# Graph attention on one core: a step's transposes and its running maximum are issued at other places

## The chip, the core and the metric

The kernel is one program on one core of a Trainium2 chip. The metric is device time in microseconds of one execution, given as the median of three runs. A profiled execution of the same program gives the trace that all views below are taken from. Engines: TensorE (PE for its matmuls, PEld for its weight loads), VectorE (DVE), ScalarE (ACT), GpSimd (POOL) and SyncE (SP).

## What is computed

Two layers over a graph of 10,000 nodes with 512 features and 160,000 edges `src -> dst`. Layer 0 is a mixture of four two-layer graph convolutions. Layer 1, where the change is, is graph attention with 8 heads of 64, followed by a feed-forward block. Cut to what matters:

```python
q, k, v = (z @ W.T + b for each)          # z = layernorm(x)
s = einsum('ehd,ehd->eh', q[src], k[dst]) / sqrt(64) + att_bias
m = segment_max(s, src);  p = exp(s - m[src])
alpha = p / segment_sum(p, src)[src]
agg = segment_sum(alpha * v[dst], src)
x = x + agg @ Wo.T + bo
x = x + silu(layernorm(x) @ W1.T + b1) @ W2.T + b2      # 512 -> 1024 -> 512
out = layernorm(layer_input + x)
```

## The kernel before, in words

The program runs three stages one after the other: the first convolutions, then the second ones with the projections to q, k and v, then attention with the feed-forward block. Only the third is touched. It starts at line 1459 of the kernel (`with ExitStack() as p3`).

**Tiling.** The nodes are cut into 79 blocks of 128 (`NB`). A block is worked off in four steps (`NQ`), each for a window of 32 nodes, so that there are 316 steps. A step `w` has block `b` and quarter `j = w % 4`. The edges of a window fill five columns of 128 slots (`CAP`): four of its own, and one that the block's windows share ("over"). For each column, GpSimd gathers 128 rows of key and value from `kv_all` with an indirect DMA (`pull`, L1552) into one of four buffers, two steps ahead. Softmax needs no exact maximum per node. The kernel takes one maximum per head and slot row, then one over all rows of the window, and subtracts that.

**The loop** (`for w in range(NW + 3)`) is a software pipeline whose order is written out by hand: `tc.manual_schedule` keeps PE, DVE, ACT and POOL in program order. A window goes through these stations:

- `expand` (L1793, TensorE): multiplies turned one-hots with the queries, so that each slot has its query row in PSUM. Two column pairs, groups 0 and 1. `expand_over` (L1801) does the same for the shared column in the last step of a block.
- `score` (L1845, DVE): queries times keys, one instruction of 128x1024 for each group. `score_over` is L1807 and L1810.
- L1882 (DVE): the sum over the 64 features of each head. Then `weigh` begins: L1695 (DVE) takes the maximum over the columns.
- `one`, the window's `weigh` in the next step. Four calls of `next(one, 1)`: L1697 (PE) turns the 128x8 maxima, L1700 (DVE, "last maximum") reduces the turned rows, L1702 (PE, two records, "its spread") multiplies the result with an identity so that all partitions hold it, and L1704 (DVE) subtracts it. The last call also issues the exponential L1707 and L1709 (ACT), and the first part of L1716 (POOL): probabilities times one-hots for columns 2 to 4, then L1721 (POOL).
- `two`, a step later: L1716 (DVE) does columns 0 and 1, L1730 (PE, 80 records of one step) forms the weighted sums, L1735/L1736 (DVE) and L1739 (ACT) divide.
- `three`, a step later still: L1741 (PE, "turned rows") turns the window's result, L1742 (ACT) copies it out. With a block's last window this call also puts the job `front(b)` at the head of the job list.
- `turn_hots(w + 2)`: four transposes L1576 (PE, "one-hots") and one copy L1579 (ACT), for the `expand` of the coming step. When `j == 2` a step begins with four more of the same kind, for the shared column of the next block (`over_t`).

L1697, L1702 and L1576 write to different columns of one PSUM bank, the tile `turns`.

**Dense work between.** What follows attention is put into jobs: `front(b)` (L1596 output projection, layer norm, L1620 transposes), `back` for two blocks (L1637, eight groups of four matmuls up, each followed by a Silu L1639 on ACT; L1647 down) and `tail` (L1655, L1659, last layer norm, L1662, store). `advance(rate)` gives jobs room: 2.6 us of dense TensorE work at the step's start (EARLY), 2.4 near its end (LATE), 0 in two places between, where only pieces without cost go on. A `back` job issues at most one group of L1637 in an `advance`. A step on TensorE before the change: EARLY pieces, L1697, expand group 0, L1702, the 80 weighted sums, expand group 1, L1741, L1576, LATE pieces.

ACT needs another function table for each of Exp (L1707), Silu (L1639) and Sqrt (L1679); an ACT_TABLE_LOAD at one of these lines is that switch.

Of the kernel before, what the change touches and what calls it, by code (L numbers as in the profile page):

```python
# [636 lines left out]
def fast(ctx: ExitStack, tc: tile.TileContext, a: dict, out: bass.AP, bad: bass.AP):  # L637
# [823 lines left out]
    with ExitStack() as p3:  # L1461
# [57 lines left out]
        def open_block(b):  # L1519
            if b >= NB:  # L1520
                return
            meta = dp.tile([P, SBC, WP], F32, name="meta", bufs=3)
            nc.sync.dma_start(meta, slots1[:, b * SBC:(b + 1) * SBC, :])
            oh = dp.tile([P, BC, 3, W], BF16, name="oh", bufs=3)
            mine = oh[:, :, 0, :].rearrange("p (q c) n -> p q c n", c=CAP)
            loc = meta[:, :SBC - 1, 1].rearrange("p (q c) -> p q c", c=SC_W)
            nc.vector.tensor_tensor(mine[:, :, :SC_W, :],
                                    loc[:, :, :, None].to_broadcast([P, NQ, SC_W, W]),
                                    iota_q[:, :, None, :].to_broadcast([P, NQ, SC_W, W]),
                                    op=ALU.is_equal)  # L1530
            nc.vector.tensor_scalar(mine[:, :, SC_W, :], iota_q, meta[:, SBC - 1, 1:2], None,
                                    op0=ALU.is_equal)
            nc.scalar.copy(oh[:, :, 1:, :], oh[:, :, 0:1, :].to_broadcast([P, BC, 2, W]))
            blocks[b] = meta, oh

        def open_query(b):
            if b < NB:
                q = dp.tile([3 * W, NQ, D], BF16, name="q")
                for t in range(3):
                    nc.sync.dma_start(q[t * W:(t + 1) * W],  # L1540
                                      q_all[b, t].rearrange("(j n) d -> n j d", n=W))
                queries[b] = q
# [15 lines left out]
        def pull_over(b):  # L1558
            if b < NB:
                fetch(kvo[b % 3], b, SBC - 1)  # L1560
# [9 lines left out]
        def turn_hots(w):  # L1570
            b, j = divmod(w, NQ)
            return turned(b, range(j * CAP, j * CAP + SC_W), "oh_t", 4)
# [182 lines left out]
        def advance(rate):  # L1755

            credit[0] = min(credit[0], 0.5) + rate
            for job in list(jobs):
                free = True
                while job.cost not in (None, STOP) and (  # L1760
                        free if job.cost == 0 else rate and credit[0] >= 0.5 * job.cost):
                    free = free and job.cost > 0
                    credit[0] -= max(job.cost, 0)
                    job.cost = next(job.steps, None)
                if job.cost == STOP:
                    job.cost = 0
                if job.cost is None:
                    jobs.remove(job)

        with tc.manual_schedule(engines={ET.PE, ET.DVE, ET.Activation, ET.Pool}):  # L1770
            for t in kvb[1:] + kvo[1:]:
                nc.vector.memset(t, 0.0)
            for b in range(2):
                open_block(b)
            open_query(0)
            pull_over(0)
            for w in range(KB):
                pull(w, range(SC_W))
            pull_over(1)
            over_t = {0: turned(0, range(SC_W, BC, CAP), "over_t", 2)}  # L1780
            hots = {w: turn_hots(w) for w in range(2)}
            one, two, three = iter(()), iter(()), iter(())
            qe, s_over = {}, {}

            GROUPS = [(0, 1), (2, 3)]

            def expand(w, g):

                if w < NW:
                    b, j = divmod(w, NQ)  # L1790
                    qe[w, g] = px.tile([P, 2, D], F32, name="qe")
                    for i, c in enumerate(GROUPS[g]):
                        nc.tensor.matmul(qe[w, g][:, i, :], hots[w][:, c, :], queries[b][:, j, :],  # L1793
                                         start=True, stop=True)

            def expand_over(b):

                if b < NB:
                    qe[b] = px.tile([P, 2, D], F32, name="qe")
                    for j in range(NQ):  # L1800
                        nc.tensor.matmul(qe[b][:, 0, :], over_t[b][:, j, :], queries[b][:, j, :],  # L1801
                                         start=(j == 0), stop=(j == NQ - 1))

            def score_over(b):
                if b < NB:
                    k = kvo[b % 3][:, :HV]
                    nc.vector.tensor_tensor(by_head(k), by_head(qe.pop(b)[:, 0, :]), by_head(k),  # L1807
                                            op=ALU.mult)
                    s = s_over[b] = dp.tile([P, H], F32, name="s_over")
                    nc.vector.tensor_reduce(s, k.rearrange("p (h d) -> p h d", h=H),  # L1810
                                            axis=AX.X, op=ALU.add)

            def bias_over(b):

                if b < NB:
                    nc.scalar.copy(kvo[b % 3][:, :HV].rearrange("p (h d) -> p h d", h=H)[:, :, DH],
                                   blocks[b][0][:, SBC - 1, 2:])

            expand_over(0)
            bias_over(0)  # L1820
            score_over(0)
            expand(0, 0)
            expand(0, 1)
            EARLY, LATE = 2.6, 2.4
            for w in range(NW + 3):
                b, j = divmod(w, NQ)
                kv = kvb[w % KB]
                last = j == NQ - 1
                if w < NW:
                    s = dp.tile([P, CAP, H], F32, name="s", bufs=3)  # L1830
                    nc.scalar.copy(s[:, SC_W, :], s_over[b])
                    nc.scalar.copy(
                        kv[:, :, :HV].rearrange("p c (h d) -> p c h d", h=H)[:, :, :, DH],
                        blocks[b][0][:, j * SC_W:(j + 1) * SC_W, 2:])
                if last:
                    bias_over(b + 1)
                if j == 2 and b + 1 < NB:
                    over_t[b + 1] = turned(b + 1, range(SC_W, BC, CAP), "over_t", 2)

                def score(g):  # L1840
                    if w < NW:
                        cs = GROUPS[g]
                        k = kv[:, cs[0]:cs[-1] + 1, :HV].rearrange("p c (h d) -> p c h d", h=H)
                        k = k[:, :, :, :DH]
                        nc.vector.tensor_tensor(  # L1845
                            k, qe.pop((w, g)).rearrange("p c (h d) -> p c h d", h=H), k,
                            op=ALU.mult)

                advance(EARLY)
                next(one, 1)
                score(0)
                next(two, 1)
                if last:
                    expand_over(b + 1)
                else:
                    expand(w + 1, 0)
                advance(0)  # L1860
                next(one, 1)
                score(1)
                next(one, 1)
                next(two, 1)
                expand(w + 1, 0 if last else 1)
                if last:
                    score_over(b + 1)
                if w >= 2:
                    pull(w - 2 + KB, range(SC_W))
                    if j == 0:  # L1870
                        pull_over(b + 1)
                next(one, 1)
                advance(0)
                next(three, 1)
                if w + 2 < NW:
                    hots[w + 2] = turn_hots(w + 2)
                if last:
                    expand(w + 1, 1)
                advance(LATE)
                first = iter(())  # L1880
                if w < NW:
                    nc.vector.tensor_reduce(s[:, :SC_W, :],  # L1882
                                            kv[:, :, :HV].rearrange("p c (h d) -> p c h d", h=H),
                                            axis=AX.X, op=ALU.add)
                    first = weigh(w, s)
                    next(first)
                next(two, 1)
                one, two, three = first, one, two
                if j == 1:
                    open_block(b + 2)  # L1890
                    open_query(b + 1)
                    open_rest(b)
            while jobs:
                advance(5.0)
# [57 lines left out]
```

## Time and profile before

| | |
|---|---|
| median of three runs | 11618.71 us (11617.09 to 11625.96) |
| profiled execution, its own time | 9845.47 us |
| its span, first to last instruction | 9843.6 us |
| mean granted TensorE clock in it | 0.987 |
| attention's 316 steps, first to last L1882 | 6986.8 to 9740.4 us, 8.74 us a step |
| in 7113 to 9740 us: PE, DVE, POOL, ACT busy | 92%, 88%, 75%, 68% |

The profiled execution is 15% shorter than the median of the runs, and lies 1.9 us around its span. The steps repeat in a cycle of eight (two blocks share one `back` job), and the cycle is steady: 36 cycles in the middle of the stage have lengths that agree within about 0.1 us. A step is 8.74 us on average, while the busiest engine is busy for 92% of it; so what counts is not a total but which wait ends last at each place of a step. In the views below, "<-" names what ended a wait. A line with PE has matmuls (a float32 matmul has two records), one with PEld the weight loads of the same instructions.

### The profile page before, as it was taken

What the parts mean: (1) busy time and instruction counts of PE and PEld (TensorE: products, weight loads), DVE (VectorE), ACT (ScalarE), POOL (GpSimd) and SP (SyncE); (2) the same over time, 40 slices, a digit from 0 to 9 for tenths busy, and PEclk for the clock granted to TensorE, in tenths of its full rate; (3) what the DMA queues carried; (4) which work ended last, traced back from release to release, by engine and by line L of the source; (5) the groups of instructions that cost most, each with busy time, mean ns of one, the idle gap of its engine ahead of it and who ended that gap; (6) DMA issues with size and microseconds to landing.
All of it is one profiled execution on the core that took longest, in us unless ns stands there. A gap on an engine that the chain in (4) does not pass through costs nothing.

```text
span 9843.6 us, 168369 instructions
## 1 busy us (share of the span) xinstructions
PE 9351.2 (95%) x63334; PEld 5440.1 (55%) x63334; DVE 5458.8 (55%) x8330; ACT 2943.9 (30%) x6062; POOL 6987.3 (71%) x6736
## 2 busy tenths in 40 slices
PE   7999999999999999899999999999799999999998
PEld 4666666666666667333333333333456565656565
DVE  7898992000100001355555555545788888888885
ACT  1111111111111111111111111111366666666665
POOL 5566666777777776677777777777577777777774
PEclk9999999999999999999999999999799999999999
DMA  6545445555555554788888888887788888888883
GB/s 216 179 153 158 156 158 158 160 157 162 158 162 163 160 165 132 262 299 297 294 303 301 291 298 297 299 302 274 227 273 278 272 275 271 272 274 270 272 276 125
DMA packets 1077230, 2263.26 MB, mean 230 GB/s; under 512 B 250526, under 2 KB 500260, under 8 KB 1075638
## 3 DMA queue, kind: packets, MB, share of 16 engines
q0 software_dynamic: 588224, 1659.68, 51.8%
q1 hardware_dynamic: 479456, 577.23, 17.0%
q10 hardware_dynamic: 8726, 15.49, 0.5%
q8 instruction: 502, 8.22, 0.3%
q14 instruction: 322, 2.64, 0.1%
HBM read 2181.26 MB, written 379.27 MB: 260 GB/s over the span
## 4 chain that ended last, share of the span: by engine, by line
PE 61%; DMA 10%; DVE 9%; ACT 8%; issue 7%; POOL 5%; POOLq 0%; ACTq 0%; DVEq 0%; SPq 0%
PE mm L1190 21%; PE mm L1200 11%; PE mm L1385 6%; DMA y<-y_tab,ix 5%; PE p_ag L1151 4%; PE bank L1647 3%; PE p_ag L1426 3%; DMA ring<-y_tab,ix 3%; PE bank L1637 2%; DVE m L930 2%; PE bank L1596 2%; POOL y L1330 2%; PE mm L1347 2%; DVE kv L1845 2%; PE sums L1730 2%
## 5 line engine op out<-in xcount | busy, mean ns | idle before, releaser
L1126 POOL DMA_INDIRECT ring<-in_x_dram,idx_t x1580 | 1901.2, 1203 | 1011.5 <-PE p_ag L1151 567.4
L1190 PE MATMUL mm<-tt,big 128*128 128x256 f32 (+1 forms) x8960 | 1964.7, 377 | 0.0
L1190 PEld LDWEIGHTS mm<-tt,big 128*128 128x128 f32 x8960 | 1680.5, 190 | 289.3 <-issue 71.3
L1060 POOL DMA_INDIRECT sorted<-pay,addr x1250 | 1278.0, 1022 | 380.5 <-issue 336.6
L1552 POOL DMA_INDIRECT kv<-kv_all,meta x948 | 965.4, 1018 | 515.6 <-PE sums L1730 276.6
L1330 POOL DMA_INDIRECT y<-y_tab,ix x920 | 950.4, 1033 | 287.2 <-issue 217.9
L1200 PE MATMUL mm<-wn,h 128*128 128x512 f32 x2528 | 1124.0, 597 | 0.0
L1385 PE MATMUL mm<-big,hb 128*128 128x512 f32 x2528 | 1120.4, 596 | 1.2 <-DMA hb<-h_tab 1.2
L1192 ACT ACTIVATE h<-mm,bl 128x256 f32<-128x256 f32 (+1 forms) x640 | 301.8, 472 | 2125.7 <-PE mm L1190 2125.7
L1330 POOL DMA_INDIRECT ring<-y_tab,ix x660 | 686.8, 1041 | 234.6 <-issue 162.7
L1347 PE MATMUL mm<-big,z_t 128*128 128x512 f32 x1896 | 829.2, 594 | 0.7 <-ACT z_t L1340 0.7
L1388 DVE TENSOR_TENSOR mine<-mm,bias 128x512 f32<-128x512 f32 x316 | 218.6, 692 | 1075.4 <-PE mm L1385 1074.9
L1385 PEld LDWEIGHTS mm<-big,hb 128*128 128x128 f32 x2528 | 468.7, 190 | 597.6 <-issue 536.1
L1200 PEld LDWEIGHTS mm<-wn,h 128*128 128x128 f32 x2528 | 468.6, 190 | 595.2 <-issue 595.0
L1637 PE MATMUL bank<-big,big 128*128 128x256 f32 (+1 forms) x2560 | 619.3, 385 | 139.8 <-ACT big L1639 139.8
L1426 PE MATMUL p_ag<-y,oh 128*32 128x512 f32 x3680 | 596.9, 605 | 83.2 <-DMA y<-y_tab,ix 83.1
L902 DVE TENSOR_TENSOR oh<-loc_t,iota_w 128x640 f32<-128x640 bf16 x158 | 131.7, 834 | 930.4 <-PE p_ag L1151 850.9
L1347 PEld LDWEIGHTS mm<-big,z_t 128*128 128x128 f32 x1896 | 361.0, 191 | 455.9 <-issue 429.0
L1647 PE MATMUL bank<-big,big 128*128 128x512 f32 x1264 | 586.6, 602 | 25.9 <-ACT big L1639 25.2
L1637 PEld LDWEIGHTS bank<-big,big 128*128 128x128 f32 x2560 | 466.2, 192 | 257.0 <-ACT big L1639 180.6
L1450 ACT ACTIVATE t<-t,gsel 128x512 f32<-128x512 f32 x158 | 109.2, 722 | 1623.5 <-DVE t L1448 1623.4
L1845 DVE TENSOR_TENSOR kv<-qe,kv 128x1024 f32<-128x1024 f32 x474 | 576.1, 1215 | 0.6 <-issue 0.6
(298 smaller groups left out, 14383.1 us busy)
## 6 DMA issues: line engine op xcount, KB each, us to landing
y_tab<-y SPq DMA_DIRECT2D x632, 256.0 KB
hb<-h_tab SPq DMA_DIRECT2D x316, 256.0 KB
h_tab<-h SPq DMA_DIRECT2D x156, 512.0 KB
kv_all<-kvt SPq DMA_DIRECT2D x79, 520.0 KB
xb<-in_x_dram SPq DMA_DIRECT2D x156, 256.0 KB
q_all<-q SPq DMA_DIRECT2D x79, 384.0 KB
q<-q_all SPq DMA_DIRECT2D x237, 128.0 KB
ring<-in_x_dram,idx_t POOLq DMA_INDIRECT x1580
```

The source lines that it names most:

```text
L1060: inst = nc.gpsimd.indirect_dma_start(out=sorted1[:], out_offset=bass.IndirectOffsetOnAxis(ap=addr_i[:, c0 + c:c0 + c + 1], axis=0), in_=p ...
L1126: nc.gpsimd.indirect_dma_start(out=gbuf[i % GB], out_offset=None, in_=x, in_offset=bass.IndirectOffsetOnAxis(ap=window(idx_t, b)[:, j, c:c ...
L1190: nc.tensor.matmul(ph[:, :n], w[:, k, f * P:(f + 1) * P], tt[:, i, k, :n], start=(i + k == 0), stop=(i == 1 and k == KD - 1))
L1200: nc.tensor.matmul(py, h[:, k, i * P:(i + 1) * P], wn[e][:, k, :], start=(k == 0), stop=(k == KD - 1))
L1330: nc.gpsimd.indirect_dma_start(out=ybuf[i % YB], out_offset=None, in_=y_flat, in_offset=bass.IndirectOffsetOnAxis(ap=ahead[b][1][:, j, c:c ...
L1347: nc.tensor.matmul(po, z_t[:, k, :], wqkv[i][:, k, :], start=(k == 0), stop=(k == KD - 1))
L1385: nc.tensor.matmul(pr, hb[:, k, :], wr[e][:, k, :], start=(k == 0), stop=(k == KD - 1))
L1426: nc.tensor.matmul(p_ag[v][j * W:(j + 1) * W, :], oh[:, j * CAP + c, :], g[:, v * D:(v + 1) * D], start=(c == 0), stop=(c == CAP - 1))
L1552: nc.gpsimd.indirect_dma_start(out=to, out_offset=None, in_=kv_all[:], in_offset=bass.IndirectOffsetOnAxis(ap=blocks[b][0].bitcast(I32)[:, ...
L1637: nc.tensor.matmul(ph, up(f, k), z_t[:, k, :m], start=(k == 0), stop=(k == KD - 1))
L1647: nc.tensor.matmul(po, hid[:, k, i * P:(i + 1) * P], w2[k // KD][:, k % KD, :], start=(k == 0), stop=False)
L1845: nc.vector.tensor_tensor(k, qe.pop((w, g)).rearrange("p c (h d) -> p c h d", h=H), k, op=ALU.mult)
```

## The change

Two edits in the loop; no instruction is added or removed in the source.

```diff
                 advance(0)
-                next(one, 1)
                 score(1)
                 next(one, 1)
                 next(two, 1)
+                next(one, 1)
                 expand(w + 1, 0 if last else 1)
...
                 next(one, 1)
                 advance(0)
+                if last:
+                    expand(w + 1, 1)
+                advance(LATE)
                 next(three, 1)
                 if w + 2 < NW:
                     hots[w + 2] = turn_hots(w + 2)
-                if last:
-                    expand(w + 1, 1)
-                advance(LATE)
                 first = iter(())
```

The first edit puts the last maximum (L1700, DVE) behind the second `score` (L1845), and its spread (L1702, PE) behind the weighted sums (L1730). The second puts the LATE dense pieces ahead of L1741 and of the four L1576, and in a block's last step `expand` ahead of both. Since `next(three, 1)` also starts `front(b)`, that job now begins at the next EARLY instead of at the same step's LATE, and the dense jobs shift by half a step against the steps. In the changed program's order a step on TensorE reads: EARLY pieces, L1697, expand group 0, the 80 weighted sums, L1702, expand group 1, LATE pieces, L1741, L1576.

## Prediction

> **What bounds the kernel now.** I read the busy time by stretches first, then the waits, then the timeline of one cycle of eight steps. The stretches (columns: window, its length, then busy us of PE, PEld, DVE, ACT, POOL; clock; DMA share; GB/s) show two engines close to full in attention and a third that is fuller than it looks, since each of POOL's gathers is followed by 0.30 us in which it issues:
>
> ```profile
> 7113.00:9740.00 2627.00, 2425.10 (x32780) 1573.29 (x32783) 2307.12 (x3733) 1795.58 (x3929) 1977.11 (x1941) 1.00 0.82 270
> ```
>
> The waits (total us, times, longest) name the places. DVE stands at the last maximum for a transpose that comes behind dense work, and TensorE's up-matmuls stand for ScalarE's Silu:
>
> ```profile
> DVE top L1700 <- PE turns L1697: 233.0, 224, 3.0
> ...
> PEld bank L1637 <- ACT big L1639: 180.6, 128, 2.4
> PE bank L1637 <- ACT big L1639: 139.8, 128, 2.1
> ...
> PEld turns L1697 <- ACT over_t L1579: 55.2, 76, 3.2
> ```
>
> The timeline (start, length) shows how such a stall is made. The LATE up-group has run on TensorE from 8029.08, but ScalarE first does the exponential, two copies and a table load; only then comes Silu, and EARLY's group, next on TensorE, waits 1.43 us:
>
> ```profile
> 8029.08 1.95 PE L1637 MATMUL bank<-big,big 128*128 128x256 f32 x8
> ...
> 8029.67 0.31 ACT L1709 ACTIVATE far<-s,spread 128x40 f32<-128x40 f32 x1
> 8029.89 0.24 ACT L1742 COPY att_t<-sums 128x128 f32<-128x128 f32 x1
> 8030.04 0.58 ACT L1579 COPY oh_t<-turns 96x512 bf16<-96x512 bf16 x1
> ...
> 8030.63 1.28 ACT L1639 ACT_TABLE_LOAD   x1
> ...
> 8031.93 0.47 ACT L1639 ACTIVATE big<-bank,b 128x256 f32<-128x256 f32 x1
> ...
> 8032.46 1.99 PE L1637 MATMUL bank<-big,big 128*128 128x256 f32 x8 [1.43 <-ACT big L1639]
> ```
>
> A third thing is who works beside whom. VectorE's L1716 takes 0.68 us alone; where it starts under GpSimd's L1716 it took up to 1.89:
>
> ```profile
> 8032.71 0.68 DVE L1716 TENSOR_TENSOR ohp<-oh,p 128x512 f32<-128x512 bf16 x1
> ...
> 8041.14 1.49 POOL L1716 TENSOR_TENSOR ohp<-oh,p 128x768 f32<-128x768 bf16 x1
> ...
> 8041.30 1.89 DVE L1716 TENSOR_TENSOR ohp<-oh,p 128x512 f32<-128x512 bf16 x1
> ```
>
> In all, 152 of the 316 are so stretched, and end 0.56 us (median) after GpSimd's.
>
> [...]
>
> **The change part by part.** I measure a step from T, the start of its L1702, to the next T, and number the steps of the cycle so that 2 and 6 end with L1801's step, 3 and 7 have five gathers, 0 and 4 end with the one-hots of the shared column. Starts in the trace give, from step 0 to 7: 9.31, 8.09, 10.05, 7.63, 9.19, 8.31, 9.12, 8.35; sum 70.05 us, and 316/8 = 39.5 cycles.
>
> *TensorE after, without a wait.* By start distances in the trace: L1702 0.32, an expand pair 0.44, L1741 and L1576 0.33, L1697 with expand and sums up to the next T 1.9: 2.99 us, plus 0.42 or 0.44 where L1801 adds a pair, 0.22 where over_t is turned, and the dense pieces of the changed order (up-group 1.73; 512-wide matmul 0.86; turned z 0.44; bias 0.22). Steps 0 to 7: 6.67, 7.31, 8.81, 8.37, 7.51, 8.38, 8.82, 6.45; sum 62.3. The same sum before was 62.1, its stalls some 7.3, and the rest is the wait at L1702. So about 8 us a cycle were to be won at most.
>
> *Second edit, gain.* Silu no longer stands behind the two copies (0.63 us by starts), and L1741 with L1576 (0.33) lie between LATE's and EARLY's up-groups. No gather and no SP DMA moves. Of L1639's table loads the changed order has 194 instead of 233; at 1.28 us this is ScalarE time, not the path.
>
> *Second edit, price.* The weighted sums (1.3 us) now stand ahead of T, so LATE's up-group ends earlier against the exponential: at T+2.49. The chain to Silu: subtraction at T+0.45 (below), its exponential and L1709 end 2.04 later as in the trace (T+2.49), table load 1.28 and Silu 0.47 with small gaps: T+4.27. TensorE would be ready at T+2.82. The stall is 1.49 us in step 7, 1.56 in step 1 (a copy L1621 comes between), and in step 0, where the shared column's L1576 stand directly behind the first four and wait for their copy (T+5.04), with another 0.2 at L1697: 2.4. Before, the corresponding stalls were 6.0 in all (0.85+1.77+0.43+1.57+0.53+0.82). In step 4 L1697 waits for the copy of over_t, which is behind L1739 (needs VectorE's L1736, T+4.6) and L1533 (1.15): T+7.62 against 6.4 on TensorE, 2.0 with its 0.8 earlier stall, partly the same: step 4 is 9.5.
>
> *First edit, gain.* VectorE's 7.4 us a cycle of idle time before L1700 have `score` (1.14) ahead of them.
> *First edit, price.* What covered the round trip L1700, L1702, L1704 was that `score`: L1704 lay 0.99 after T. Now nothing does, except in steps 2 and 6 (score_over, 1.4). The trace never shows the trip bare. One transpose to L1700 takes 0.38; two records take 0.13 more; bounds 0.38 and 0.70, taken 0.45. Behind a waiting L1704 stand L1603/L1655, L1606/L1659 and L1882. VectorE's path from T to T: 0.45, L1704 0.10, L1882 2.35, L1695 to L1736 0.40, two scores 2.27, L1716 0.60, L1700 with its hand-over 0.35: 6.51 (by starts), plus norm pieces 1.3 in steps 7, 3 and 4, small ones 0.1 to 0.4, one-hot pieces 0.8 in steps 0 and 4.
> And L1716's place: GpSimd's begins 7.04 us after the sums' start in the five-gather steps 3 and 7, so at T+5.74, and ends at 7.24. VectorE's would begin at 6.1 (step 7) and 5.84 (step 3), end 0.56 after GpSimd's, and cost 1.0 to 1.3 more; VectorE then needs 9.15. [...] Bounds: 0 and 1.3 for each.
>
> *Sum, the longest path of each step 0 to 7:* 9.09, 8.87, 8.81, 9.1, 9.5, 8.38, 8.82, 9.15 = 71.7. Against 70.05 this is +1.7 us a cycle, x 39.5 = +67 us on the profiled execution (9845.47, of it 9843.6 span): about 9912.
>
> **From there to the median.** Nothing in the views says why the runs take 11618.71. If the rest is a fixed addition, +67 stays; if everything is stretched by 11618.71/9845.47 = 1.18, it is +79. [...] I take +72: **11690 us**, +0.6%.
>
> **The rivals.**
> - *The filler does what it is put there for (faster).* Mechanism: LATE's Silu runs under L1741 and L1576, and VectorE's lost cover costs nothing since VectorE is ahead. For it: 7.4 us of VectorE's idle time a cycle. Against: the exponential's 2.04 us and the table load lie ahead of Silu. Without overlap at L1716 and without over_t's wait, steps 3, 7, 4, 0 become 8.4, 8.2, 9.1, 8.6: 69.2, -0.9 x 39.5 = -36; with the free ends of the bounds 67.6: -97. Middle: 11555. It decides if the bare trip is under 0.4 us and VectorE's L1716 stays clear in steps 3 and 7.
> - *It cancels (same).* One of the two L1716 overlaps is absent and over_t's wait halves: about 70.1, 11620.
> - *The lost cover costs in every step (slower by more).* The trip is 0.70 and L1716 overlaps in 6 steps: +3.5 a cycle, 11757 and up. VectorE is then the bound.
> - *The dense jobs shift otherwise than meant.* They do shift by half a step; that is in the sums, and a case of the above.
>
> **How the numbers follow.** Forecast 0.47, slower by more 0.14, same 0.16, faster 0.23. About 0.2% (23 us) is what a measurement of this kernel can tell from no change. So faster 0.23, same 0.16, slower 0.61. The forecast's own range is 11650 to 11735; since the other side holds 0.23, the range of 8 in 10 reaches from 11565 into it, and to 11770 above.
>
> **What would show it.** Right: VectorE's wait before L1700 nearly gone and one before L1704 in its place, mostly on L1702; L1637's waits on L1639 still some 100 us; L1697's on L1579 up; more or longer stretched L1716 on VectorE in the five-gather steps. Wrong: no wait before L1704, L1637's waits under 60 us, TensorE over 94% busy in the stage.

## The result

| | median of the runs | ratio to before |
|---|---|---|
| before | 11617.9 us (20 runs, 11561.18 to 11664.72) | |
| after | 11700.11 us (20 runs, 11619.65 to 11753.68) | 1.0071 (1.0053 to 1.0089) |

Slower by 0.7%: +82 us, where +72 was forecast. The number is right, but the working behind it is not, as a repetition under the conditions of the profile of before shows (+266 us, four times the working's +67).

The reason that both can be: the same program was seen in two conditions. Either the kernel before takes about 9830 us (its profile, 9845.47, is such an execution) or some 11,560 to 11,740 us (all its timed runs above are such, and so is the profile of after: its own time 11728.03, span 11726.2). Within each set of runs on one chip all runs were in the same condition; what settles it is not known. I call the two quick and slow supply, for a reason that the trace shows below. Ratios in this text are always between runs of one chip.

The stretches of after (window, length, then busy us of PE, PEld, DVE, ACT, POOL; clock; DMA share; GB/s), over its attention stage:

```profile
7723.00:11625.00 3902.00, 3023.60 (x34208) 1856.81 (x34208) 2342.76 (x3897) 1835.79 (x4034) 1981.61 (x2030) 0.89 0.59 190
```

TensorE is busy for 77%, where the profile of before had 92%. Attention takes 12.4 us a step and not 8.74, and also the two stages ahead of it, which the change doesn't touch, are longer (attention begins at 7723 us and not at 6987). So the two pages may not be subtracted. The waits of after (total us, times, longest) answer to the forecast's list:

```profile
DVE s L1704 <- PE qe L1793: 870.9, 199, 6.6
...
PEld sums L1730 <- issue: 476.7, 1002, 1.3
...
DVE den L1735 <- ACT att_t L1742: 246.3, 172, 3.3
...
PEld bank L1637 <- ACT big L1639: 191.8, 89, 3.4
```

VectorE's wait before L1700 is gone and stands before L1704, as forecast, but it is longer than the old one by far (870.9 us in this line and 1260.7 in all at L1704, against 233 before); and TensorE's sums wait for nothing that the profile shows ("issue"), 1002 times. The timeline of one step (start, length; x is the count of records that are drawn together) shows what that is:

```profile
9501.43 0.29 DVE L1700 TENSOR_REDUCE top<-turns 128x1 f32<-128x128 f32 x1
...
9501.76 1.11 PE L1730 MATMUL sums<-kv,ohp 128*32 128x65 f32 x64
...
9503.79 0.33 PE L1730 MATMUL sums<-kvo,ohp 128*32 128x65 f32 x5 [0.40 <-issue]
...
9504.52 0.34 PE L1730 MATMUL sums<-kvo,ohp 128*32 128x65 f32 x5 [0.40 <-issue]
...
9504.78 0.28 PE L1702 MATMUL turns<-ident,top 128*128 128x8 f32 x1
...
9506.96 0.20 DVE L1704 TENSOR_TENSOR s<-s,turns 128x40 f32<-128x40 f32 x1 [5.24 <-PE qe L1793]
```

The first 64 matmuls run off in 1.11 us. The last ones come five at a time, 0.73 us apart (9503.79 to 9504.52): five weight loads and five matmuls, so 73 ns a record. The maximum was ready at 9501.72, and its spread L1702, now behind the sums, starts 3.06 us later. Its second record starts at 9505.26, and L1704 only 1.70 us after that; the profile names an L1793 for this rest and doesn't say what held it. Over all steps the 80 matmuls start within 2.9 us (median) here, and under quick supply, in either kernel, within 1.2.

### The profile page after: what moved, and what is told of

It reads as the page before. It is cut to its first block, busy times and chain, and to the rows that moved or that the text cites. A ratio compares the mean times of both kernels' runs of the same rounds, so it can differ in the third digit from the quotient of the medians.

```text
span 11726.2 us, 168401 instructions
## 1 busy us (share of the span) xinstructions
PE 10195.1 (87%) x63334; PEld 5754.0 (49%) x63334; DVE 5367.0 (46%) x8330; ACT 2922.2 (25%) x6022; POOL 6901.0 (59%) x6736
## 4 chain that ended last, share of the span: by engine, by line
PE 73%; issue 8%; DVE 6%; ACT 6%; another core or an unknown queue 4%; DMA 2%; POOL 1%; ACTq 0%; SPq 0%; POOLq 0%; DVEq 0%
PE mm L1190 18%; PE mm L1200 9%; PE mm L1385 8%; PE p_ag L1426 6%; PE mm L1347 6%; PE sums L1730 4%; PE bank L1637 4%; PE p_ag L1151 4%; PE bank L1647 3%; PE qe L1793 3%; PE bank L1596 3%; DVE m L930 2%; ACT L1707 1%; ACT L1639 1%
## 5 line engine op out<-in xcount | busy, mean ns | idle before, releaser
L1190 PE MATMUL mm<-tt,big 128*128 128x256 f32 (+1 forms) x8960 | 2027.0, 383 | 66.7 <-issue 63.3
L1385 PE MATMUL mm<-big,hb 128*128 128x512 f32 x2528 | 1210.4, 623 | 107.3 <-issue 96.1
L1347 PE MATMUL mm<-big,z_t 128*128 128x512 f32 x1896 | 876.3, 615 | 151.0 <-DVE mine L1388 112.7
L1637 PE MATMUL bank<-big,big 128*128 128x256 f32 (+1 forms) x2560 | 729.2, 436 | 204.9 <-ACT big L1639 176.1
L1647 PE MATMUL bank<-big,big 128*128 128x512 f32 x1264 | 668.9, 662 | 71.4 <-DVE x L1655 70.8
L1637 PEld LDWEIGHTS bank<-big,big 128*128 128x128 f32 x2560 | 545.4, 222 | 349.7 <-ACT big L1639 191.8
L1704 DVE TENSOR_TENSOR s<-s,turns 128x40 f32<-128x40 f32 x316 | 62.1, 196 | 1260.7 <-PE qe L1793 870.9
```

The lines of the kernel that those rows point to most:

```text
L1190: nc.tensor.matmul(ph[:, :n], w[:, k, f * P:(f + 1) * P], tt[:, i, k, :n], start=(i + k == 0), stop=(i == 1 and k == KD - 1))
L1347: nc.tensor.matmul(po, z_t[:, k, :], wqkv[i][:, k, :], start=(k == 0), stop=(k == KD - 1))
L1385: nc.tensor.matmul(pr, hb[:, k, :], wr[e][:, k, :], start=(k == 0), stop=(k == KD - 1))
L1637: nc.tensor.matmul(ph, up(f, k), z_t[:, k, :m], start=(k == 0), stop=(k == KD - 1))
L1647: nc.tensor.matmul(po, hid[:, k, i * P:(i + 1) * P], w2[k // KD][:, k % KD, :], start=(k == 0), stop=False)
```

## The experiments

**The change again, beside its own before.** First on one chip, with nothing edited in either kernel.

> The kernel before, unchanged, for a second profiled execution. If the profiled execution of before on the page (9845 us) was peculiar in how fast TensorE got its instructions, this one lies near the timed median, 11,600 us, its attention steps near 12 us as in the profile after (12.38 us), and the weighted sums show gaps that end in 'issue'. If the change itself made those gaps, this one shows 8.74 us a step again.

> The changed kernel, unchanged: +0.7% (11,690 to 11,710 us) as in its first runs. A second profile tells how far two profiles of one program differ: if near 9,900 us, the recorded theory's +67 us can be compared with the profile of before directly.

The chip had quick supply. The kernel before took 9831.46 us, ratio 1.000 (0.9992 to 1.0009) to 17 other runs of it, and its steps are those of the forecast's working (70.05 us is the sum of the steps' medians; single cycles of the first trace last from 69.6 to 73.0). The changed kernel took 10097.08 us: 1.0278 (1.0264 to 1.0292), +266 us. The medians of its eight steps add up to 77.07 us; (77.07 - 70.05) x 39.5 = +277, and with means, 76.86 against 70.20, +263. So the cycle holds the whole difference. The stretches of the changed kernel on this chip, in the window that the forecast showed for before:

```profile
7113.00:9740.00 2627.00, 2230.90 (x29912) 1436.36 (x29910) 2224.14 (x3417) 1636.93 (x3557) 1817.51 (x1779) 0.99 0.75 250
```

TensorE falls from 92% to 85%, at nearly the same clock: it is made to wait. Its waits say for what:

```profile
DVE s L1704 <- PE turns L1702: 269.2, 241, 3.3
...
PEld turns L1697 <- ACT over_t L1579: 154.9, 77, 4.8
DVE den L1735 <- ACT att_t L1742: 154.6, 156, 2.2
PEld bank L1637 <- ACT big L1639: 135.2, 90, 2.2
...
PE turns L1576 <- ACT oh_t L1579: 99.5, 79, 2.0
```

All but that of L1735 were in the forecast. L1735 forms the softmax's denominators. It reads the PSUM tile `sums`, L1742 copies other columns of the same tile, and L1735 waits for that copy (7 us in all before, 155 now). L1742 belongs to "turned rows", which stand behind LATE's pieces. The timeline of such a step:

```profile
8212.94 1.28 ACT L1639 ACT_TABLE_LOAD   x1
...
8214.23 0.47 ACT L1639 ACTIVATE big<-bank,b 128x256 f32<-128x256 f32 x1
8214.61 0.26 ACT L1742 COPY att_t<-sums 128x128 f32<-128x128 f32 x1
...
8214.90 0.16 DVE L1735 TENSOR_SCALAR den<-sums 128x2 f32<-128x2 f32 x1 [1.34 <-ACT att_t L1742]
...
8215.17 0.69 DVE L1527 TENSOR_TENSOR oh<-meta,iota_q 128x512 bf16<-128x512 f32 x1
...
8216.16 1.26 ACT L1533 COPY oh<-oh 128x1280 bf16<-128x1280 bf16 x1 [0.35 <-DVE rs L1683]
...
8217.54 0.57 ACT L1579 COPY over_t<-turns 96x512 bf16<-96x512 bf16 x1
...
8218.17 0.33 PE L1697 MATMUL turns<-ident,wide 128*128 128x128 f32 x1 [0.61 <-ACT over_t L1579]
```

Read downward: table load and Silu, then the copy L1742, then VectorE's L1735 (1.34 us late) and, behind it, L1527, which makes one-hots of a coming block; then ScalarE's L1533, which copies these one-hots and so waits for VectorE (the profile names L1683, the instruction that ended last there); then the copy of over_t, and only then TensorE's L1697. Next keys stand behind L1735 on VectorE as well.

**Each edit alone**, same chip.

```diff
# edit1_maximum: the first edit
-                next(one, 1)
                 score(1)
                 next(one, 1)
                 next(two, 1)
+                next(one, 1)
# edit2_turns, and edit2_again on another chip: the second
+                if last:
+                    expand(w + 1, 1)
+                advance(LATE)
                 next(three, 1)
                 if w + 2 < NW:
                     hots[w + 2] = turn_hots(w + 2)
-                if last:
-                    expand(w + 1, 1)
-                advance(LATE)
```

> First edit alone: the last maximum behind the second keys, its spread behind the weighted sums. Recorded theory (cover lost on VectorE, L1716 beside GpSimd's): +20 to +80 us, with a wait before L1704 of 0.4 to 0.7 us a step. Rival theory (TensorE's instruction supply: L1702 has to wait until 160 records of the sums are issued, and the exponential, GpSimd's L1716 and the next sums with it): it carries all of the loss, +80 us or more, with a wait before L1704 of 2 us and more a step.

> Second edit alone: LATE's dense pieces ahead of the turned rows and one-hots. Recorded theory: Silu no longer behind two copies, so a gain of 20 to 70 us; its price, the sums ahead of T, belongs to the first edit. Rival theory (the turn of the shared column's one-hots directly behind the first four, and the job shift): a loss of 10 to 40 us, with longer waits of L1576 on L1579.

The first alone: 10086.22 us, 1.0259 (1.0244 to 1.0273). The second alone: 10095.17 us, 1.0269 (1.0255 to 1.0283). Each costs nearly as much as both together, so the costs don't add. Neither theory of the second's expectation came near, and the first lost what its rival theory had, but with 1.0 us a step at L1704 and not the 2 that were to go with it. In the waits of the first edit alone, and then of the second alone:

```profile
DVE s L1704 <- PE turns L1702: 310.4, 242, 3.3
```

```profile
PEld turns L1702 <- DVE top L1700: 287.4, 311, 2.6
...
DVE den L1735 <- ACT att_t L1742: 261.4, 238, 4.2
...
PEld turns L1697 <- ACT over_t L1579: 177.0, 77, 3.2
```

Each makes VectorE late by a way of its own: at L1704 the first, at L1735 the second (whose L1700 then comes too late for TensorE). After that both end at the same place: L1697 on over_t is 166.3 us with the first edit alone, 177.0 with the second, 154.9 with both, 55.3 with neither.

**The halves of each edit.** The next four kernels start from before.

```diff
# hots_behind (and hots_behind_again): only the one-hots behind LATE
                 next(three, 1)
-                if w + 2 < NW:
-                    hots[w + 2] = turn_hots(w + 2)
                 if last:
                     expand(w + 1, 1)
                 advance(LATE)
+                if w + 2 < NW:
+                    hots[w + 2] = turn_hots(w + 2)
# rows_behind: only the turned rows behind LATE
-                next(three, 1)
                 if w + 2 < NW:
                     hots[w + 2] = turn_hots(w + 2)
                 if last:
                     expand(w + 1, 1)
                 advance(LATE)
+                next(three, 1)
# max_vector_only: L1700 behind the second keys, L1702 ahead of the sums
-                next(one, 1)
                 score(1)
                 next(one, 1)
+                next(one, 1)
                 next(two, 1)
# spread_tensor_only: L1700 ahead of the second keys, L1702 behind the sums
                 next(one, 1)
                 score(1)
-                next(one, 1)
                 next(two, 1)
+                next(one, 1)
```

> From before, one half of the second edit: only the one-hots' transposes (L1576) and their copy L1579 go behind LATE; L1741 and L1742 stay ahead of it, and front(b) starts where it did. Theory of the copies (in the two step-ends where the shared column's L1576 follow directly, TensorE waits for L1579, and L1697 later for the second L1579): +30 to +110 us against before, L1697's waits on L1579 from 55 to above 120 us. Theory of the divide (what costs is L1742 late, because L1735 waits for it): at most +30 us, L1735's waits on L1742 near nothing.

> From before, the other half: only next(three), L1741 with its copy L1742 and the start of front(b), goes behind LATE; the one-hots stay ahead. Theory of the divide (L1742 reads the PSUM tile that L1735 reads too, stands behind LATE's Silu, and L1735 stands ahead of the next keys on VectorE): most of the loss, +150 to +270 us, L1735's waits on L1742 above 150 us as in the second edit alone (261 us). Theory of the copies: within +60 us.

> From before, one half of the first edit: L1700 goes behind the second L1845 on VectorE, but L1702 stays ahead of the 80 weighted sums on TensorE. Theory of the lost cover (the round trip L1700, L1702, L1704 is bare): +120 to +260 us, VectorE waits 0.5 us a step at L1704, and TensorE waits at L1702 for L1700 in nearly every step (130 us before, 300 or more here). Theory of the place behind the sums: within +50 us.

> From before, the other half: L1700 stays ahead of the second L1845, but L1702 goes behind the weighted sums. Theory of the place behind the sums (1.3 us of sums, which wait for VectorE's and GpSimd's L1716, ahead of the maximum): +150 us or more, waits at L1704 of 150 us and more. Theory of the lost cover: the score still covers the trip, at most +60 us, and VectorE's waits at L1700 for L1697 are as before (233 us).

This chip had slow supply: before took 11718.71 us here (11 runs).

| | us | ratio (95%) |
|---|---|---|
| hots_behind | 11515.2 | 0.9835 (0.9816 to 0.9854) |
| rows_behind | 11554.8 | 0.9856 (0.9836 to 0.9875) |
| max_vector_only | 11762.43 | 1.0041 (1.0025 to 1.0056) |
| spread_tensor_only | 11941.37 | 1.0178 (1.0164 to 1.0192) |

The expectations had counted in stalls of the quick condition. For the first edit's halves the theory of the place behind the sums came (+223 us and +44 us, where it had 150 or more and at most 50). For the second's no theory had a gain of this size: both gain, rows_behind too, although L1735 waits there for L1742 for 1168.2 us in all. Of the first edit, the place of L1702 is what costs most. The waits of spread_tensor_only:

```profile
DVE s L1704 <- PE sums L1741: 1029.9, 254, 5.6
```

L1704 waits 1029.9 us in this line for a TensorE on which the spread stands behind sums that come slowly; max_vector_only, with the spread ahead of them, has 119.6 us at that place. A second part comes after the sums: L1704 starts 2.25 us (median) after L1702 in spread_tensor_only, and 0.42 in max_vector_only.

**A second repetition:** the kernel before once more, and the second edit beside it.

> The kernel before once more, for a profile. Theory of TensorE's instruction supply: where its time is near 11,600 to 11,700 us, its 80 sums L1730 take about 3.6 us instead of 1.2, its attention steps about 12.3 us, and VectorE's L1704 waits little, since L1702 stands ahead of the sums. Where its time is near 9,830 us, it repeats the profile before. The change cannot be the cause of slow sums if they show here.

> Second edit alone. Where before takes about 11,700 us: theory of supply, 1.5 to 2.5% faster, like each of its halves there (0.9835 and 0.9856)[...]; theory of the divide, slower, as where before takes 9,830 us (1.0269). Where before takes 9,830 us: 1.027 again.

This third chip had quick supply again: before_third 9831.92 us, 1.000 (0.9991 to 1.0009), edit2_again 10089.32 us, 1.0258 (1.0244 to 1.0272). So there is no trace of the kernel before under slow supply; the second run repeats edit2_turns.

**Shorter sums, and the one-hots where supply is quick.**

```diff
# short_sums: the changed kernel, without columns 2 and 3 in the sums L1730
-            for c in range(CAP):
+            for c in (0, 1, CAP - 1):
```

> The changed kernel with the weighted sums over columns 0, 1 and the shared one alone: columns 2 and 3 are left out of L1730, so that a step has 48 records of it instead of 80; all else runs, GpSimd's and VectorE's L1716 over all columns too. Theory of supply: where before takes about 11,700 us, L1704 no longer waits for late sums (871 us in the profile after), and the time falls by 3% or more below the changed kernel, to 0.975 of before or less. Where before takes 9,830 us, the sums take 0.7 instead of 1.2 us and supply is no limit: 1.013 to 1.028 of before.

> Only the one-hots' transposes behind LATE, as before. Where before takes 9,830 us: theory of the divide (the second edit's 1.027 comes from L1742 behind LATE, for which L1735 waits), 0.995 to 1.008, with L1735's waits on L1742 below 60 us. Theory of the copies (the second edit's loss comes from L1576 and L1697 waiting for L1579): 1.010 to 1.027, with L1697's waits on L1579 above 120 us. Where before takes about 11,700 us: 0.984 again.

With 48 records in place of 80 ahead of L1702, the changed kernel still took 10064.32 us: 1.0236 (1.0222 to 1.025). The length of the sums is therefore not what most of the 2.8% is made of where supply is quick (a kernel before with shorter sums was not run beside it). The wait of L1704 on L1702 falls from 269.2 to 167.4 us, L1735's rises from 154.6 to 178.5, and the time hardly moves.

hots_behind_again took 9817.25 us against 9832.41: 0.9985 (0.9978 to 0.9992), a gain of 15 us, as the theory of the divide had it. Its waits, beside those of the second edit alone above:

```profile
PEld bank L1637 <- ACT big L1639: 72.5, 91, 2.3
...
PEld turns L1697 <- ACT over_t L1579: 36.9, 77, 3.3
...
DVE den L1735 <- ACT att_t L1742: 28.2, 45, 2.0
```

The four L1576 behind LATE do what a filler is for: L1637's waits for Silu fall from 180.5 to 72.5 us, and L1735 stays free since L1741 and L1742 stay ahead of LATE. So what costs is the rest of the second edit, `next(three, 1)` behind LATE as well: with it 1.0269, without it 0.9985. (Alone, as rows_behind, it was run under slow supply only.) It is one call with two effects, since it holds L1741 and L1742 and also starts `front(b)` half a step later; no run took the two apart.

## Why the number was right and its working not

**Step by step, quick supply.** The time from T to T in us (medians over 36 cycles in the middle of the stage), and what TensorE's weight loads waited for on other engines in the changed kernel (means; at L1576 the median wait of its matmuls):

| step | forecast | measured | TensorE's main waits |
|---|---|---|---|
| 0 | 9.09 | 10.69 | L1576 on its copy 2.04, L1697 on over_t 1.53 |
| 1 | 8.87 | 8.97 | L1637 on Silu 1.55 |
| 2 | 8.81 | 8.81 | none over 0.4 |
| 3 | 9.1 | 9.11 | L1730 on ScalarE's L1679 1.11, by the profile |
| 4 | 9.5 | 10.69 | L1697 on over_t 2.19, L1647 on VectorE's L1655 0.93 |
| 5 | 8.38 | 8.60 | L1730 on ScalarE's L1639 0.60, by the profile |
| 6 | 8.82 | 9.89 | L1596 on VectorE's L1655 1.30 |
| 7 | 9.15 | 10.31 | L1637 on Silu 1.56, L1793 on VectorE's L1845 1.42 |

The four steps 0, 4, 6 and 7 give 5.0 of the 5.4 us by which the cycle is longer than forecast.

- *Right:* the bare trip. L1704 starts 0.42 us after T, taken 0.45. The stalls for Silu in steps 7 and 1: 1.56 and 1.55, taken 1.49 and 1.56. In step 0, 2.04 at L1576 against the forecast's 2.2. The stretched L1716 in the five-gather steps: 35 of 36 in step 3 (1.92 us, and the step is 9.11) and 14 of 36 in step 7, where before had one in all 72. L1639's table loads: 194, each of 1.28 us (in before there is one at each of the 657 changes between L1707, L1639 and L1679, and none at a repetition). Steps 1, 2, 3 and 5 hold within 0.25.
- *The step that failed:* VectorE's path from T to T. Three of its terms were too small: "L1695 to L1736 0.40", the one-hot and small pieces (0.8, and 0.1 to 0.4), and L1655, which got no price for those who wait for it.
- *First term, "L1695 to L1736 0.40".* It has L1735 without a wait, as it was before. The second edit moves L1742 behind a table load and a Silu, and L1735, which reads `sums` too, waits for it: 1.35 us in step 0, 1.79 in step 1, 0.43 in step 2. It is the kind of wait that the forecast named for `turns` and L1697, at a second tile; the forecast asked only at the first. In step 1 it cost next to nothing. In step 0 it goes on by way of L1527, L1533 and over_t to L1697: 1.53 there, where the forecast had 0.2.
- *Second term, the one-hot and small pieces.* The forecast let GpSimd's L1716 collide with VectorE's L1716 alone. It also struck other VectorE instructions that the shifted schedule put beside it. The groups of the changed kernel (count, then busy us and mean ns of one):

```profile
L1716 DVE TENSOR_TENSOR ohp<-oh,p 128x512 f32<-128x512 bf16 x316 | 356.0, 1127 | 0.0
L1527 DVE TENSOR_TENSOR oh<-meta,iota_q 128x512 bf16<-128x512 f32 x79 | 126.7, 1604 | 0.0
...
L1684 DVE SCALAR_TENSOR_TENSOR rs<-mv,rs 128x1 f32<-128x1 f32 x158 | 73.5, 465 | 5.4
```

Before, on the same chip, they had 362.3, 55.0 and 29.4 us: L1527 and L1684 lost 116 us. Step 4 shows the first of them. L1735 doesn't wait, but L1527 meets GpSimd's L1716 and takes 1.81 us instead of 0.69, and ScalarE's L1533 waits for the one-hots that it makes:

```profile
7866.17 0.15 DVE L1735 TENSOR_SCALAR den<-sums 128x2 f32<-128x2 f32 x1
7866.19 1.49 POOL L1716 TENSOR_TENSOR ohp<-oh,p 128x768 f32<-128x768 bf16 x1
...
7866.43 1.81 DVE L1527 TENSOR_TENSOR oh<-meta,iota_q 128x512 bf16<-128x512 f32 x1
...
7868.55 1.26 ACT L1533 COPY oh<-oh 128x1280 bf16<-128x1280 bf16 x1 [1.48 <-DVE rs L1683]
```

The copy of over_t then ends at T+8.67 (median), where the forecast had T+7.62; that is nearly the whole excess of step 4 (10.69 against 9.5), and L1527 was stretched there in each of 35 cycles (1.82 us, the median). In step 0, L1735's wait pushes L1527 into the same place: stretched in 28 of 36 cycles, with a step of 10.70 us, against 9.90 in the other eight. For step 7 the timeline shows the other line:

```profile
8203.86 2.22 DVE L1684 SCALAR_TENSOR_TENSOR rs<-mv,rs 128x1 f32<-128x1 f32 x1
...
8204.57 1.48 POOL L1716 TENSOR_TENSOR ohp<-oh,p 128x768 f32<-128x768 bf16 x1
...
8206.00 1.21 DVE L1845 TENSOR_TENSOR kv<-qe,kv 128x1024 f32<-128x1024 f32 x1
...
8207.27 0.61 PE L1793 MATMUL qe<-q,oh_t 96*128 96x512 bf16 x2 [1.96 <-DVE kv L1845]
```

A one-element-per-row instruction of 0.16 us takes 2.22, the keys come late, and TensorE's next expansion stands 1.96 us for the buffer that they read. Here the cycles of one run decide: in 15 of 36 L1684 got through in 0.16 us, and step 7 took 9.14 us (median), the forecast's 9.15; in the 21 others L1684 took 2.2 and the step 10.54. Both kinds begin about 0.7 us ahead of GpSimd's L1716, those that get through 0.01 us or so earlier. So, by this comparison, the collision is what lengthens step 7. In the view VectorE's starts first and yet ends with GpSimd's (starts on GpSimd are rough in this profile), while GpSimd's own L1716 takes 1.48 to 1.50 us in all 316 steps of this run. The trace of before had such cases too: 12 of its 152 stretched L1716 begin ahead of GpSimd's and take 2.1 to 3.5 us, where the forecast's reading was "starts under" and "up to 1.89".

Time lost so by the three lines (their busy time above 0.68, 0.69 and 0.16 us for one) is 152 us in before, 164 in hots_behind_again, and 262 to 305 in the changed kernel, the two with one edit each, and short_sums: high in all that lose where supply is quick. No run took the contention away, so how much of the 2.8% is its own, and how much the waits at L1735 and L1704 that lead to it, is not settled.
- *Third term, L1655.* In step 4 it stands behind the waiting L1704, in step 6 behind L1810 and L1704, and TensorE waits for the bank that it empties (0.93 and 1.30). In step 6 this is the one long wait, and the step is 1.07 over the forecast; in step 4 TensorE waits for over_t anyway.

**The rivals.** "The filler works" was to decide by a trip under 0.4 us and an L1716 that stays clear in steps 3 and 7. The trip was at its edge (0.42), and L1716 was not clear. But the condition left out what mattered: in the second edit the filler comes together with the delay of L1742. Taken alone (hots_behind) it does make the kernel faster. "Lost cover in every step", with a trip of 0.70, is refuted by the 0.42.

**From there to the runs.** The forecast took +72 since "nothing in the views says why the runs take 11618.71". This was the place where the error was made up for, by luck: not by that figure, but because the timed runs were of the other condition. In the profile of after the sums take two and a half times as long, a step has 12.4 us, and two prices of the table nearly vanish: L1697's weight load waits for over_t 25.2 us in all, and only 39 of VectorE's L1716 are stretched. There the place of L1702 costs (+1.8% for spread_tensor_only, +0.4% for max_vector_only), and each half of the second edit gains (-1.65%, -1.44%). A loss of 2.2% by the first edit and a gain of 1.5% by the second would give the recorded +0.7%, but that is not shown: the two halves of the second together would gain 3.1%, and all four halves added give -0.9%. Neither edit as a whole was run under slow supply, and the halves plainly need not add. Under slow supply the change cost less (+0.7%) than under quick (+2.8%).

**Open.** Why the supply differs is not settled. The clock (0.936 in the profile of after, 0.988 in before_again) is too small a difference for sums that are two and a half times as long. No run shows what makes the 73 ns a record in the step shown (146 ns for a weight load with its matmul). Nor can 73 ns be the rate of all records, since attention as a whole has one in 57 ns. What keeps L1704 for some 2 us after L1702 has started is open as well.

**Better than both kernels:** hots_behind, 0.9985 of before where supply is quick and 0.9835 where it is slow. Only the four L1576 and their copy move behind LATE; L1741, L1742 and the maximum stay.

## What to carry to other kernels

When work is moved past dense pieces, follow its last instruction, often a small copy, and ask for each engine that shares a PSUM tile with it what then waits (here L1735, 155 us in all), and not only at the tile that the edit is about. If a profile's own time is 15% off the timed runs, a sum worked out on it forecasts another machine; first find which instructions are longer, and give the forecast both answers. GpSimd's L1716 (1.48 us, two inputs) held up VectorE's L1716, L1527 and L1684 in each of 594 cases in which they began up to 0.69 us ahead of it, even one that takes 0.16 us alone, so after a shift ask which instruction now stands there.

## What the runs showed of the hardware

- One program, the kernel before, ran at two speeds: 9830 to 9833 us on three chips, 11718.71 on a fourth, with every run of a set alike. In the step shown under slow supply the last records of the sums come 73 ns apart after the first 64 matmuls. In attention as a whole (the profile of after), 68416 records in 3902 us are one in 57 ns.
- Prices change with it: under slow supply the turned rows behind LATE and the one-hots behind LATE gained 1.4% and 1.7%, each alone; under quick supply both together lost 2.7%, the one-hots alone gained 0.15%.
- A VectorE instruction of 128x1 took 2.22 us at GpSimd's 1.48 us L1716, and 0.16 alone. Counted over all 14 traces, L1716, L1527 and L1684 on VectorE (both inputs in SBUF) were stretched in 594 of 594 cases when they began up to 0.69 us ahead of GpSimd's L1716, in 25 of 78 between 0.69 and 0.72 us, and in none of 545 from there to 1.3 us. Those of 128x512 end 0.56 us after GpSimd's, those of 128x1 0.03. L1845, L1603 and L1655, which read one operand from PSUM, were stretched in none of 847 cases in the first of these places.
- VectorE's L1735 reads columns of the PSUM tile `sums`, ScalarE's L1742 other columns of it, and L1735's wait for L1742 went from 7 us in all (before) to 261 (edit2_turns).
